# Second attention in pairs of chunks with its weighted sums added up by VectorE, and a rearranged start of the first attention

## The chip, the cores and the metric

The kernel runs on one core of a Trainium2 chip. A core has five engines with instruction streams of their own: TensorE (PE; its weight loads, PEld, overlap its matmuls), VectorE (DVE), ScalarE (ACT), GpSimd (POOL) and SyncE (SP), which here only issues transfers. Work is ordered within an engine; between engines a semaphore makes one wait for another. TensorE writes to PSUM, a memory of 8 banks with 128 partitions of 512 fp32 each; the other engines read it from there.

The metric is the time of the kernel on the device in microseconds, the median over its runs; lower is better.

## The reference

A network over 128 queries of 256 features (x), with 12544 context rows of 256 features (ctx) in its two attentions:

```
ln = layernorm without weights
x = x + cross_attention(ln(x), ctx, mask)   # 4 heads of 64: softmax(q k^T / 8, masked) v Wo
x = x + gated_delta_net(ln(x))              # 12 heads, convolutions of 4, a scan over the 128 rows
x = x + top1_of_8_experts(ln(x))
x = x + cross_attention_16(ln(x), ctx)      # 16 heads of 16, with biases: softmax(q k^T / 4) v
x = x + gated_linear_attention(ln(x))       # phi = elu + 1, running sums with a decay per head
x = x + top2_of_8_experts(ln(x))
```

All is float32. The change touches the two cross attentions alone. The second one computes, for each head h and context row c, e[c, s] = exp(q[s] . k[c] / 4 + a shift of the query), then out[s] = (sum over c of e[c, s] v[c]) / (sum over c of e[c, s]).

## The kernel before

The context is taken in 25 blocks: 24 of 512 rows and one of 256, 98 chunks of 128 rows. Everything is laid out with context rows on partitions and queries along the free axis, so that exp(scores) goes into the weighted sum without a transposition.

The order of the whole is: the first attention (`xattn0_first`), `delta_net`, `experts`, the second attention's queries and shifts (`xattn1_first`), its main loop (`weigh1`), `last_layers`. Keys and values of the second attention depend on the context alone; they are computed in small units (`keys1`, `values1`) which an object `Filler` hands out between other work of TensorE: `fill(n)` emits the next n units, `into` tells them which PSUM pool to use. The last two values units are kept for the start of `weigh1`, where `last` gives them one PSUM bank to write to. Each values unit pair ends with a copy from PSUM (L1067, ScalarE). The program also contains a second network for the case that the first attention's sums overflow; with these data it is not run.

**Order of instructions.** In a region under `manual_schedule` the named engines run in the order in which the code is written; the others (POOL and SP, and DVE where it is not named) are ordered by the framework's scheduler. The first attention has PE, ACT and DVE by hand, the rest PE and ACT. Where two instructions share a tile of a pool, the later one waits by semaphore for those that used it before.

**First attention.** PSUM is held by two pools: `x0_mm` with three tiles of two banks each (`two(name)`), opened first, and `x0_ot` with one bank for the output sums and one spare for the twelve warming matmuls of L387. At the start the layer norm of x is computed while PE does keys(0); then come two transposes (`ln_pt`, L167), the query projection (`pq`, L501), ACT's scaled copy to `qT` (L505), masked maxima of block 0's scores (L515, DVE L518), values(0) (L433), DVE's diagonal of the negative maxima (L526), keys(1) (L420), and a matmul with ones that spreads the maxima (`pn`) to `nm` (L530). The loop takes two blocks at a time, b and b+1. In PE's order: values of the two blocks before; keys of the two new blocks (L420); the weighted sums of the two blocks before (`weigh`, L481); the scores of the two new blocks (L454). Each block has two tiles `e` of 256 context rows by 4 heads. DVE adds `nm` to the scores (L460), ACT takes Exp (L461), POOL converts the 0/1 mask from uint8 (`mk`, L463) and multiplies `e` by it (L467). DVE adds each `e` to `sums` (`add_up`, L472), one round later. At the end the result `x_xattn` is added up by DVE (L586) from a tile of `x0_mm`; delta_net opens pools of its own in the same banks, the fillers' among them.

**Second attention (`weigh1`).** PSUM: `st_a` and `st_b`, three banks each, `st1` and `ot`, one bank each: 8 in all. `scores(i)` makes the scores of chunk i for 16 heads: 16 matmuls of K = 32 (four heads' strips side by side, j = 0 to 3, in groups g), three quarters into `st_a` or `st_b` by turns, the fourth (j = 0) into `st1`. ACT takes Exp of `st1` (512 columns) and then of the three-bank tile (1536 columns) into an SBUF tile `e`, of which there are three. `attend(i)` makes 16 matmuls that write 17 partitions each (16 features of v and a one for the denominator), in four column strips. All 98 attends accumulate in the one bank `ot`, which a matmul with zeros (L1157) opens. In PE's order: scores(0), the last values units, scores(1), then for every i scores(i+2) and attend(i). So each chunk changes twice between the two kinds of matmul. The keys of block b+2 are loaded to SBUF by SP (`load1`) when block b begins; `late` loads the weights of the last layers at block 12. After the loop ACT copies `ot` to SBUF in two halves (L1162), PE transposes it (L1165) into `st1`, and DVE takes the reciprocal (L1168) and multiplies.

Each of these fp32 matmuls appears in the profile as two PE records, so a pass of 16 has 32.

Of the kernel before, what the change touches and what calls it, by code (L numbers as in the profile page):

```python
# [23 lines left out]
S = 128  # L24
# [48 lines left out]
def network(ctx: ExitStack, tc: tile.TileContext, a: dict, y_out, bad):  # L73
# [291 lines left out]
    def xattn0_first(ahead, ok, filler, rest):  # L365
# [5 lines left out]
        with (  # L371
# [3 lines left out]
            tc.tile_pool(name="x0_s", bufs=1) as sp,  # L375
            tc.tile_pool(name="x0_mm", bufs=3, space=PSUM) as ps_mm,
            tc.tile_pool(name="x0_ot", bufs=1, space=PSUM) as ps_ot,
# [48 lines left out]
            def values(b):  # L426
                vs[b] = kvp.tile([128, 4, D], F32, tag="v", name="v")
                pv = two("pv")
                for i in range(BLOCKS[b][1] // 256):
                    for c in range(2):  # L430
# [12 lines left out]
            def scores(b):  # L443
# [4 lines left out]
                for c0 in range(0, n // 128, 2):  # L448
# [18 lines left out]
                    nc.gpsimd.tensor_mul(e, e, mk.unsqueeze(1).to_broadcast([128, 4, 2, S]))  # L467
# [28 lines left out]
            hT = layernorm(x, ps_one, "mm", lambda n: keys(0) if n == 4 else None)  # L496
            qT = wp.tile([128, 2, S], F32, name="qT")
            pq = two("pq")
            for m in range(2):
                for k in range(KC):  # L500
                    nc.tensor.matmul(  # L501
                        pq[:, m, :S], wq[:, k, m * 128 : (m + 1) * 128], hT[:, k, :],
                        start=(k == 0), stop=(k == KC - 1),
                    )
            nc.scalar.mul(qT, pq[:, :, :S], DH**-0.5)  # L505
# [16 lines left out]
            values(0)  # L522
# [529 lines left out]
    def values1(b, where):  # L1052
# [4 lines left out]
        for c0 in range(0, n // 128, 2):  # L1057
            pv = where.tile([128, 2, D], "pv")
            for c in range(2):
# [6 lines left out]
                if c == 1:  # L1066
                    nc.scalar.copy(v[:, c0 : c0 + 2, :, :16], pv.rearrange("p c (h d) -> p c h d", h=16))  # L1067
# [10 lines left out]
    def weigh1(x, qs, kss, cp, sp, loaded, late, rest=None):  # L1078
# [3 lines left out]

        H, DH, G = 16, 16, 4
        with (
# [6 lines left out]
            nc.gpsimd.tensor_scalar_mul(turned[:, :NE], row[:, ROW["bg"]], -1.0)  # L1091
            nc.gpsimd.tensor_scalar(turned[:, NE:], row[:, ROW["iota"]], -1.0, 64.0, ALU.mult, ALU.add)
# [5 lines left out]
            zl = cp.tile([1, 128], BF16, name="zl")  # L1098
            nc.gpsimd.memset(zl, 0.0)
            zr = cp.tile([1, 512], BF16, name="zr")  # L1100
            nc.gpsimd.memset(zr, 0.0)

            ws = [ep.tile([128, 4, G, S], F32, name=f"e{n}") for n in range(3)]


            st_b = ps_sb.tile([128, 3, G, S], F32, name="st_b")
            ot = ps_st.tile([128, G, S], F32, name="ot")
            st1 = ps_st.tile([128, 1, G, S], F32, name="st1")
            st_a = ps_st.tile([128, 3, G, S], F32, name="st_a")

            def scores(i):
                b, c = chunks[i]
                e, st3 = ws[i % 3], (st_a, st_b)[i % 2]
                for g in range(G):
                    for j in (1, 2, 3, 0):
                        r = slice(32 * j, 32 * j + 32)
                        nc.tensor.matmul(  # L1117
                            st3[:, j - 1, g, :] if j else st1[:, 0, g, :],
# [3 lines left out]
                for st, j in ((st1, slice(0, 1)), (st3, slice(1, 4))):  # L1122
                    nc.scalar.activation(  # L1123
                        e[:, j].rearrange("p j g s -> p (j g s)"),
                        st.rearrange("p j g s -> p (j g s)"), AF.Exp,
                    )
                return e

            def attend(i, e):
                b, c = chunks[i]  # L1130
                v = val_blocks[b]
                for g in range(G):
                    for j in range(4):
                        nc.tensor.matmul(  # L1134
                            ot[32 * j : 32 * j + DH + 1, g, :],
                            v[:, c, 8 * (g // 2) + 2 * j + g % 2, :], e[:, j, g, :],
                            start=False, stop=(i + 1 == len(chunks) and g == G - 1),
# [3 lines left out]
            for b in range(loaded, 2):  # L1141
                load1(kss, b)
            with tc.manual_schedule(engines={PE, ACT}):
                es = [scores(0)]
                if rest:
                    rest(ot)
                es.append(scores(1))
# [611 lines left out]
```

## Time and profile before

| what | value |
|---|---|
| median of 3 runs | 759.05 us (758.59 to 759.15) |
| profiled execution | 759.24 us |
| its span in the profile | 757.4 us, clock of TensorE 0.998 of full speed |
| first attention, 0 to 288 us | PE busy 284.5 us |
| layer norm to the end of the experts and queries, 288 to 515 us | PE busy 224.4 us |
| main loop of the second attention, 515 to 726 us | PE busy 209.7, ACT 191.6, DVE 0.65, POOL 0.00 us |
| last layers, 726 us to the end | PE busy 22.1 us of 31 |

The span runs from the first to the last instruction that the profiler recorded, on one execution; the execution's own time is 1.84 us longer. A row of the page's groups says: line of the kernel, engine, operation, output tile and input tiles, shapes (partitions x elements; for matmuls rows*columns of the array), count, then busy time, mean of one in ns, and the idle time of the engine before these instructions with what ended it. A row of the timeline has the start in us, the duration, the engine, line and operation, and in brackets the idle time before it. Durations of neighbouring PE rows overlap, since matmuls are pipelined; the distance of two starts is what PE needed.

### The profile page before, as it was taken

How to read it: one execution, taken by the hardware profiler on the slowest of the kernel's cores; microseconds unless marked ns; L12 is line 12 of the kernel's file. 1: busy time of each engine (PE TensorE's matmuls, PEld its weight loads, DVE VectorE, ACT ScalarE, POOL GpSimd, SP SyncE). 2: the span in 40 equal slices, each digit the busy share in tenths (PEclk: the TensorE clock that was granted, in tenths of full speed). 3: DMA queues.
4: the chain of work that ended last, by engine and by line, in shares of the span. 5: the costliest groups of instructions: out<-in, count | busy, mean ns of one | idle time of the engine just before them, and what ended most of it. 6: DMA issues, size and time to landing. Idle time of an engine off the chain costs nothing.

```text
span 757.4 us, 23122 instructions
## 1 busy us (share of the span) xinstructions
PE 740.8 (98%) x10473; PEld 556.5 (73%) x10473; DVE 224.9 (30%) x421; ACT 397.0 (52%) x483; POOL 234.4 (31%) x192
## 2 busy tenths in 40 slices
PE   8999999999999999999999999999999999999985
PEld 4677777777777777666677666667888888888873
DVE  3454444345444434983123251000000000000045
ACT  1433343344334323473235223337999999999951
POOL 5586666677666650506012030000000000000000
PEclk9999999999999999999999999999999999999999
DMA  9970000000000002324111453211432222222000
GB/s 319 379 286 8 5 8 9 8 8 4 8 9 3 1 29 79 107 98 140 46 43 43 149 135 120 83 70 59 141 105 66 69 59 70 70 66 68 10 2 12
DMA packets 36123, 56.65 MB, mean 75 GB/s; under 512 B 5904, under 2 KB 12608, under 8 KB 36016
## 3 DMA queue, kind: packets, MB, share of 16 engines
q1 hardware_dynamic: 35648, 54.05, 22.0%
q8 instruction: 84, 1.38, 0.8%
q0 software_dynamic: 368, 1.03, 0.4%
q14 instruction: 23, 0.19, 0.1%
HBM read 42.09 MB, written 12.98 MB: 73 GB/s over the span
## 4 chain that ended last, share of the span: by engine, by line
PE 95%; POOL 2%; DVE 1%; ACT 1%; issue 1%; POOLq 0%; DVEq 0%; ACTq 0%
PE ot L1134 13%; PE pk L1041 11%; PE pv L1062 11%; PE pv L433 11%; PE pk L420 10%; PE st_b L1117 7%; PE st_a L1117 7%; PE st L454 6%; PE ot L481 6%; PE pr L650 1%; POOL e L467 1%; PE py L970 1%; PE st L1117 1%; PE pg L780 1%; PE py L1494 1%; PE pout L944 1%
## 5 line engine op out<-in xcount | busy, mean ns | idle before, releaser
L467 POOL TENSOR_TENSOR e<-e,mk 128x1024 f32<-128x1024 f32 x49 | 115.4, 2355 | 77.2 <-ACT e L461 71.8
L1117 PE MATMUL st<-qs,ks 32*128 32x128 f32 x784 | 113.0, 283 | 0.5 <-ACT e L1123 0.5
L1134 PE MATMUL ot<-e,ctx 128*17 128x128 f32 x3136 | 104.7, 274 | 0.0
L1117 PEld LDWEIGHTS st<-qs,ks 32*128 32x128 f32 x784 | 94.4, 186 | 0.7 <-ACT e L1123 0.7
L1041 PE MATMUL pk<-ctx,wk 128*128 128x512 f32 (+1 forms) x200 | 92.6, 589 | 0.0
L1062 PE MATMUL pv<-wv,ctx 128*128 128x256 f32 x384 | 90.1, 382 | 1.2 <-ACT kh L1048 0.6
L472 DVE TENSOR_TENSOR sums<-sums,e 128x1024 f32<-128x1024 f32 x49 | 60.0, 1225 | 100.7 <-POOL e L467 100.7
L433 PE MATMUL pv<-wkv,ctx 128*128 128x256 f32 x392 | 88.3, 383 | 0.0
L1062 PEld LDWEIGHTS pv<-wv,ctx 128*128 128x128 f32 x384 | 71.7, 190 | 22.0 <-issue 10.7
L420 PE MATMUL pk<-ctx,wkv 128*128 128x512 f32 (+1 forms) x200 | 86.4, 583 | 0.0
L1134 PEld LDWEIGHTS ot<-e,ctx 128*17 128x17 f32 x3136 | 77.5, 97 | 12.1 <-ACT e L1123 0.3
L461 ACT ACTIVATE e<-e 128x1024 f32<-128x1024 f32 x49 | 51.8, 1057 | 65.2 <-DVE e L460 62.4
L433 PEld LDWEIGHTS pv<-wkv,ctx 128*128 128x128 f32 x392 | 73.3, 190 | 11.7 <-PE sc L515 0.8
L1123 ACT ACTIVATE e<-st_a 128x1536 f32<-128x1536 f32 x49 | 70.8, 1445 | 0.0
L1123 ACT ACTIVATE e<-st_b 128x1536 f32<-128x1536 f32 x49 | 70.8, 1445 | 0.0
L463 POOL TENSOR_SCALAR mk<-msk 128x256 f32<-128x256 uint8 x49 | 68.2, 1393 | 4.1
L460 DVE TENSOR_TENSOR e<-st,nm 128x1024 f32<-128x1024 f32 x49 | 56.6, 1217 | 40.9 <-PE st L454 40.9
L420 PEld LDWEIGHTS pk<-ctx,wkv 128*128 128x128 f32 x200 | 38.1, 190 | 40.8 <-issue 40.0
L1123 ACT ACTIVATE e<-st 128x512 f32<-128x512 f32 x98 | 58.5, 597 | 17.0 <-PE st L1117 17.0
L1048 ACT ACTIVATE kh<-pk,col 128x512 f32<-128x512 f32 (+1 forms) x50 | 33.8, 679 | 63.4 <-PE pk L1041 62.3
L1168 DVE RECIPROCAL den<-st 128x16 f32<-128x16 f32 x1 | 0.3, 257 | 209.2 <-PE st L1165 209.2
L1117 PE MATMUL st_a<-qs,ks 32*128 32x128 f32 x1176 | 57.3, 283 | 0.0
(333 smaller groups left out, 850.2 us busy)
## 6 DMA issues: line engine op xcount, KB each, us to landing
ctx<-in_ctxT SPq DMA_DIRECT2D x24, 512.0 KB, 7.9
kd<-kh SPq DMA_DIRECT2D x48, 256.0 KB, 2.0
ks<-kd SPq DMA_DIRECT2D x192, 64.0 KB, 2.8
w<-in_L_ffn_expert_w SPq DMA_DIRECT2D x4, 512.0 KB, 3.9
ctx<-in_L_ffn_We SPq DMA_DIRECT2D x4, 512.0 KB, 3.9
msk<-in_maskT SPq DMA_DIRECT2D x24, 64.0 KB, 1.8
w<-in_L_attn_Wqk SPq DMA_DIRECT2D x2, 768.0 KB, 9.8
w<-in_L_attn_Wv SPq DMA_DIRECT2D x2, 768.0 KB, 12.1
```

The lines of the kernel that those rows point to most:

```text
L420: nc.tensor.matmul(pk[:, m, :n], wkv[:, k, m * 128 : (m + 1) * 128], ctx_blocks[b][:, k, :], start=(k == 0), stop=(k == KC - 1),)
L433: nc.tensor.matmul(pv[:, i, c * D : (c + 1) * D], ctx_blocks[b][:, k, rows], wkv[:, k, D:], start=(k == 0), stop=(k == KC - 1),)
L460: nc.vector.tensor_add(e, st, nm.unsqueeze(2).to_broadcast([128, 4, 2, S]))
L461: nc.scalar.activation(e, e, AF.Exp)
L463: nc.gpsimd.tensor_scalar(mk, msk[:, c0 * 128 : (c0 + 2) * 128].rearrange("p (c s) -> p c s", c=2), 1.0, 0.0, ALU.mult, ALU.add,)
L467: nc.gpsimd.tensor_mul(e, e, mk.unsqueeze(1).to_broadcast([128, 4, 2, S]))
L472: nc.vector.tensor_add(sums, sums, e)
L1041: nc.tensor.matmul(pk, wk1[:, k, m * 128 : (m + 1) * 128], ctx_blocks[b][:, k, :], start=(k == 0), stop=(k == KC - 1),)
L1062: nc.tensor.matmul(pv[:, c, :], ctx_blocks[b][:, k, rows], wv1[:, k, :], start=(k == 0), stop=(k == KC - 1),)
L1117: nc.tensor.matmul(st3[:, j - 1, g, :] if j else st1[:, 0, g, :], kss[b % 3][r, g // 2, g % 2, c * 128 : (c + 1) * 128], qs[r, g, :], star ...
L1123: nc.scalar.activation(e[:, j].rearrange("p j g s -> p (j g s)"), st.rearrange("p j g s -> p (j g s)"), AF.Exp,)
L1134: nc.tensor.matmul(ot[32 * j : 32 * j + DH + 1, g, :], v[:, c, 8 * (g // 2) + 2 * j + g % 2, :], e[:, j, g, :], start=False, stop=(i + 1 = ...
```

## The change

In the **second attention** two chunks make a pair, 49 in all. Pair p: scores of chunks 2p and 2p+1, then the attends of the pair before, 2p−2 and 2p−1. There is no bank `ot` any more. Two single banks `ones` change roles: the pair's first chunk puts its j = 0 quarter into `first`, the second chunk into `second`; once ACT has read `first`, the two attends write their sums there, the first of them with start=True. DVE adds the bank to an accumulator `acc` in SBUF (copies it for the first pair). In the next pair the two banks change places. The last pair has four attends. There are four tiles for the Exps rather than three; the fourth large one lies in a slot of the ring of weights. The memsets and the matmul that opened `ot` are gone, and ACT's two copies at the end; the transposes read `acc`. The last values units of the filler are copied by VectorE rather than ScalarE, and sit between the first two pairs. Since a slot of the ring is taken, the two loads of `L1_attn_W` (768 and 512 KB) stand one set of keys later in SP's order.

In the **first attention** the pools are opened in the other order, so that `x0_ot` has the first two banks. values(0) is split into two halves (a generator, `value_steps`): the first is emitted after the layer norm's transposes, the second after the query projection. The transposed rows and the query projection share one two-bank tile, and both halves of the projection lie in one bank. The mask multiplication of the last tile of every odd block (12 of 49) goes to VectorE.

```diff
+            tc.tile_pool(name="x0_ot", bufs=1, space=PSUM) as ps_ot,
             tc.tile_pool(name="x0_mm", bufs=3, space=PSUM) as ps_mm,
-            tc.tile_pool(name="x0_ot", bufs=1, space=PSUM) as ps_ot,
...
             def values(b):
+                for _ in value_steps(b):
+                    pass
+
+            def value_steps(b):
                 vs[b] = kvp.tile([128, 4, D], F32, tag="v", name="v")
                 pv = two("pv")
                 for i in range(BLOCKS[b][1] // 256):
+                    if i > 0:
+                        yield
                     for c in range(2):
...
-                    nc.gpsimd.tensor_mul(e, e, mk.unsqueeze(1).to_broadcast([128, 4, 2, S]))
+
+                    engine = nc.vector if b % 2 == 1 and c0 + 2 == n // 128 else nc.gpsimd
+                    engine.tensor_mul(e, e, mk.unsqueeze(1).to_broadcast([128, 4, 2, S]))
...
-            hT = layernorm(x, ps_one, "mm", lambda n: keys(0) if n == 4 else None)
+            first = value_steps(0)
+            shared = two("shared")
+
+            class Half:
+                def tile(self, shape, dtype, tag, name):
+                    return shared[:, 0, :]
+
+            def between(n):
+                if n == 4:
+                    keys(0)
+                elif n == 1:
+                    next(first)
+
+            hT = layernorm(x, Half(), "mm", between)
...
-            pq = two("pq")
+            pq = shared[:, 1, :].rearrange("p (m s) -> p m s", m=4)
...
+            nc.scalar.mul(qT, pq[:, :2, :], DH**-0.5)
+            for _ in first:
+                pass
...
-            values(0)
...
-                    nc.scalar.copy(v[:, c0 : c0 + 2, :, :16], pv.rearrange("p c (h d) -> p c h d", h=16))
+                    where.copy(v[:, c0 : c0 + 2, :, :16], pv.rearrange("p c (h d) -> p c h d", h=16))
...
-            ws = [ep.tile([128, 4, G, S], F32, name=f"e{n}") for n in range(3)]
...
-            st_b = ps_sb.tile([128, 3, G, S], F32, name="st_b")
-            ot = ps_st.tile([128, G, S], F32, name="ot")
-            st1 = ps_st.tile([128, 1, G, S], F32, name="st1")
-            st_a = ps_st.tile([128, 3, G, S], F32, name="st_a")
...
+            three_b = ps_sb.tile([128, 3, G, S], F32, name="st_b")
+            ones = [ps_st.tile([128, 1, G, S], F32, name=f"one{n}") for n in range(2)]
+            three_a = ps_st.tile([128, 3, G, S], F32, name="st_a")
...
-                            ot[32 * j : 32 * j + DH + 1, g, :],
-                            v[:, c, 8 * (g // 2) + 2 * j + g % 2, :], e[:, j, g, :],
-                            start=False, stop=(i + 1 == len(chunks) and g == G - 1),
+                            one[32 * j : 32 * j + DH + 1, 0, g, :],
+                            v[:, c, 8 * (g // 2) + 2 * j + g % 2, :], e3[:, j - 1, g, :] if j else e1[:, 0, g, :],
+                            start=start and g == 0, stop=stop and g == G - 1,
...
-                es = [scores(0)]
-                if rest:
-                    rest(ot)
-                es.append(scores(1))
-                for i, (b, c) in enumerate(chunks):
+                for p in range(np_):
+                    first, second = ones[p % 2], ones[1 - p % 2]
+                    b, c = chunks[2 * p]
...
-                    if i + 2 < len(chunks):
-                        es.append(scores(i + 2))
-                    if i == 0:
-
-                        nc.tensor.matmul(ot.rearrange("p g s -> p (g s)"), zl, zr, start=True, stop=False)
-                    attend(i, es.pop(0))
-
-            oT = cp.tile([128, G, S], F32, name="oTs")
-            for g in (0, 2):
-                nc.scalar.copy(oT[:, g : g + 2], ot[:, g : g + 2])
-            pt = st1[:, 0].rearrange("p g s -> p (g s)")
+                    scores(2 * p, first, three_a)
+                    scores(2 * p + 1, second, three_b)
+                    if p == 0:
+                        if rest:
+                            rest(first[:, 0])
+                        continue
+                    attend(2 * p - 2, first, True, False)
+                    attend(2 * p - 1, first, False, p + 1 < np_)
+                    if p + 1 == np_:
+                        attend(2 * p, first, False, False)
+                        attend(2 * p + 1, first, False, True)
+                    if p == 1:
+                        nc.vector.tensor_copy(acc, first[:, 0])
+                    else:
+                        nc.vector.tensor_add(acc, acc, first[:, 0])
+
+            pt = ones[np_ % 2][:, 0].rearrange("p g s -> p (g s)")
...
+            self.copy = nc.scalar.copy
...
+            self.copy = nc.vector.tensor_copy
```

## The prediction, made before the changed kernel was run

> **What bounds the kernel now.** I read the page first, then the table of stretches, then the timeline of the second attention, and last the idle places of TensorE (PE) in the first attention.
>
> ```profile
> span 757.4 us, 23122 instructions
> PE 740.8 (98%) x10473; PEld 556.5 (73%) x10473; DVE 224.9 (30%) x421; ACT 397.0 (52%) x483; POOL 234.4 (31%) x192
> PE 95%; POOL 2%; DVE 1%; ACT 1%; issue 1%; POOLq 0%; DVEq 0%; ACTq 0%
> ```
>
> PE is busy 98% of the span and holds 95% of the chain that ended last. But the average hides stages, and busy PE is not PE at its peak. The stretch from 515 to 726 us, the second attention, has the columns PE, PEld, DVE, ACT, POOL:
>
> ```profile
> 515.00:726.00 211.00, 209.72 (x6287) 175.95 (x6285) 0.65 (x4) 191.61 (x202) 0.00 (x0) 1.00 0.24 69
> ```
>
> PE is full there, ScalarE (ACT) nearly (192 of 211), VectorE (DVE) and GpSimd (POOL) do nothing, and the clock is 1.00. One chunk on PE in the timeline (start, duration):
>
> ```profile
> 522.54 0.39 PE L1117 MATMUL st_b<-qs,ks 32*128 32x128 f32 x3
> 522.75 0.28 PE L1117 MATMUL st_b<-qs,ks 32*128 32x128 f32 x3
> ...
> 523.42 0.28 PE L1117 MATMUL st_b<-qs,ks 32*128 32x128 f32 x3
> 523.64 1.07 PE L1134 MATMUL ot<-e,ctx 128*17 128x128 f32 x32
> 524.64 0.39 PE L1117 MATMUL st_a<-qs,ks 32*128 32x128 f32 x3
> ```
>
> A score pass has 8 rounds of row strips: 0.21 from first to second, then one each 0.112 us (six to 523.42), and 0.22 to the attend pass. That has 8 rounds of column strips, 0.11 apart, and is followed after 1.00 us by the next scores. So one chunk takes 2.10 us; over the steady part (scores of chunk 4 at 524.64, of chunk 96 at 718.10) it is 193.46/92 = 2.103, or 4.206 for two chunks. Where two score passes touch (519.23, 519.35) they are 0.112 apart, as inside a pass: changing the kind of pass is what costs. ACT beside it:
>
> ```profile
> 519.59 0.60 ACT L1123 ACTIVATE e<-st 128x512 f32<-128x512 f32 x1 [0.55 <-PE st L1117]
> 520.08 1.45 ACT L1123 ACTIVATE e<-st_b 128x1536 f32<-128x1536 f32 x1
> 521.43 0.60 ACT L1123 ACTIVATE e<-st 128x512 f32<-128x512 f32 x1
> ...
> 523.84 0.60 ACT L1123 ACTIVATE e<-st 128x512 f32<-128x512 f32 x1 [0.47 <-PE st L1117]
> ```
>
> The small Exp starts 1.30 after its scores do (522.54 to 523.84); the large one 0.49 later; the next small one follows 1.35 after that when it need not wait (520.08 to 521.43), and 1.61 in the steady state, where it waits 0.16 for PE. The page's group of small Exps waits 17.0 us in all for PE: ACT has only that much to give.
>
> **The change, part by part.**
>
> *Second attention, the loop.* Per pair, PE alone would need: scores 0.21 + 14×0.112 + 0.22 = 2.00, attends 16×0.11 + 0.12 = 1.88, together 3.88 against 4.206, since of four changes of kind two are left. That saves 0.326×46 = 15.0 us over the 46 pairs from chunk 4 to chunk 96. It holds only if nothing else waits, so I follow each bank. With S the start of a pair's first score pass and S' of its second: S waits for the large Exp two chunks back (its three banks), S' for the large Exp of the pair before, and for the DVE addition that empties the single bank. Exps run in order small, large, small, large. From S: 1.30 to the first small Exp, 0.49 to the large, 1.35 to the second small, 0.49 to the second large, 1.45 its duration, 0.05 from an ACT end to PE (520.19 to 520.24): the next S' is not before S+5.13. The next S follows S' by 0.21+6×0.112+0.22+1.88 = 2.98, since a pass that has waited pays 0.21 for its first round again (520.24 to 520.45). Twice the period is therefore 8.11, the period **4.055**: Exps, not PE, set it. The attends write into the bank of the pair's first small Exp, done at S+1.95 with the way to PE; they come at S+2.28 and don't wait. Bounds: 4.00 if the waiting pass pays no 0.21, 4.09 if the large-to-small step is 1.41, as one other row has it. At 4.055 the loop saves 0.151×46 = **6.9**.
>
> "TensorEngine Tiling (Array Packing)", section Key Properties, says that a change of tiling mode drains TensorE, and by that rule alone half as many changes would be worth 49×0.32, some 16 us by estimate. The same page's section PSUM Bottleneck speaks against counting that: emptying PSUM may become the limit after packing; by it only the 6.9 of the Exp chain are had.
>
> *The DVE addition.* 47 additions and a copy, none of which was there. Rows: adding a 128x512 PSUM tile to one in SBUF took 0.69 (L1217):
>
> ```profile
> 458.53 0.69 DVE L1217 TENSOR_TENSOR qs<-qs,pm 128x512 f32<-128x512 f32 x1 [2.10 <-PE pm L1213]
> ```
>
> From PE's last matmul to the reader 0.33 to 0.40 passes (attend end 724.28, its reader 724.61). The addition is thus done about 0.9 after the next S, and S' is wanted 1.07 after S at period 4.055: 0.15 of slack, so it costs nothing. Its cover is the first score pass; without it each 0.1 late costs 4.6 us. Nothing else is queued on DVE there.
>
> *Entry and end.* The 0.50 wait for an Exp in the second scores (520.24) goes, since the last values units now lie between the first and second pair, and a switch goes; followed through the same recurrence, chunk 4's scores start at 523.3 instead of 524.64: **1.3**, bounds 0.5 (that wait alone) and 1.4 (with its repeated round of 0.21 and two switches of 0.33). At the end two ACT copies (first 0.38 before the second is done, together 0.65) give way to one addition of 0.69 before the transposes: **−0.1**. The last values copies move from ACT to DVE, 0.69 against 0.68, beside PE; the dropped memsets and the zero matmul (one round) are nothing; the moved POOL pair of small scalings keeps its place in POOL's order. The two late SP loads of last-layer weights (768 and 512 KB) come one keys set later; they are wanted after 726 and DMA is 0.24 busy, so nothing. Keys are loaded as far ahead as before.
>
> *First attention, start.* PE idles twice around the query projection:
>
> ```profile
> 11.26 1.16 PE L501 MATMUL pq<-hT,w 128*128 128x128 f32 x8 [0.52 <-DVE hT L168]
> 12.89 1.99 PE L515 MATMUL sc<-kT,qT 64*128 64x512 f32 x8 [0.47 <-ACT qT L505]
> ```
>
> The two halves of values(0), 16 instructions of 3.72 in all, move into both holes. 10.47+1.86 = 12.33 for pq, 0.86 of pq, 1.86 of the second half, scores at 15.05, 1.9 for them: keys(1) at 16.95 instead of 18.37: **1.4**. Lower bound 1.0 (0.52+0.47, the idle marks alone). Later than before comes DVE's maximum (four of 0.69) and the diagonal (1.24): ready at about 20.07, and its matmul, after keys(1) of 3.6, comes at 20.4. The second half's weights landed at 8.2, so the first half does not wait for them.
>
> *Mask multiplications to DVE.* POOL holds up PE once, in the first blocks:
>
> ```profile
> 40.50 1.10 PE L481 MATMUL ot<-e,v 128*64 128x128 f32 x16 [0.50 <-POOL e L467]
> ```
>
> 12 of 49 multiplications (2.36 each on POOL) go to DVE, where the nearest row, the sums with two SBUF inputs, is 1.225. DVE gains 12×1.225 = 15 of its 268 us with 120 busy. The multiplication stands before the sums on DVE, and waits for ACT's Exp and POOL's mask conversion; behind it queue the sums, which nobody awaits until the end, and the next scores' additions, 9 us off. In the steady state PE runs 21.38 us for two blocks without a wait, so the only gain is this stall: 41.52 to about 40.8, **0.7**; bounds 0 and 0.73.
>
> POOL's mask conversion takes 1.44 beside a sums addition and 0.39 without (0.77 for two at 16.84). "SBUF — State Buffer", section Who interferes with whom, says that a DVE instruction with two SBUF inputs contends with GpSimd's reads: the multiplication on DVE would hold up POOL's by up to 1.2 or be held by 2.36. By the rule, the tile is ready up to 2.4 later; it is wanted some 4 us later, so the sum stays.
>
> *Swapped pools.*
>
> ```profile
> 288.95 1.32 PE L1062 MATMUL pv<-wv,ctx 128*128 128x256 f32 x5 [0.60 <-DVE x_xattn L586]
> ```
>
> Delta net's first fillers now take banks that only PE's earlier work had, not the one that DVE still reads. The layer norm's result is there at 293.09, its transposes at 296.77 in PE's order: PE's work sets the time, so **0.6** goes; lower bound 0, if another reader of the banks comes late.
>
> Sum: 6.9+1.3−0.1+1.4+0.7+0.6 = **10.8**. The profiled execution took 759.24, span 757.4 and 1.84 around it, 0.19 over the median of 759.05. 759.24−10.8 = 748.4, on the median's footing **748.3**; span 746.6.
>
> **Rivals.**
>
> (a) PE alone sets the pair, because Exps pack tighter than these rows. For: ACT's rows sum to 3.68 for four. Against: the latency 1.30 after S. 15.0+3.9 = 18.9 off: 740.1.
>
> (b) Exps do not pack: large-to-small stays at 1.61, as nearly every row has it. The next S' is then S+5.39, the period 4.185, the loop saves 1.0, in all 4.9: 754.1. Against: 0.16 of the 1.61 is a wait for PE in the profile.
>
> (c) Slower: the DVE addition comes late. The period is 2.98 plus the time from S to its end. At 0.9 it would be 3.88 and hidden; at 1.06 it decides; at 1.31 (0.41 late) the period is 4.29, which eats the 3.9 of the other parts. With 0.5 late 4.38: 46×0.174 = 8.0 lost, 3.9 won, 763.2. For: an addition each pair between uses of one bank, which the profile never shows. Against: adding from PSUM took 1.217 for 1024 columns in all 49 cases beside busy PE and ACT (L460), the same rate.
>
> (d) The change moves nothing: only if the switches do not fall away; against it stands the 0.112 of adjoining passes.
>
> **How the numbers follow.** Forecast 0.68, (a) 0.08, (b) 0.12, (c) 0.08, (d) and others 0.04. The forecast's own range: periods of 4.00 to 4.09 give 9.5 to 5.3; the rest 3.9 down to 2.2 (values, stall and pools at their lower bounds): 745.7 to 751.6. The range for 8 in 10 reaches half way to (a) (period 3.95: 11.8+3.9 off, 743.4) and over (b) with the rest at 2.2 (1.0+2.2 off, 755.8). 0.2%, 1.5 us, is what a measurement tells from no change: faster 0.88 (forecast, a, b), same 0.03, slower 0.09 (c and 0.01 of the others).
>
> **What would show it.** In the second attention: starts of every second score pass 4.05 apart; rows of 64 attend instructions of one kind; the small Exps waiting for PE at one of two, some 0.28 each (large Exp ended at S+1.02, the next needed at S+1.30), 13 in all; a wait of about 0.1 for ACT's e before the second score pass of a pair, none for DVE's acc; DVE's additions near 0.69. In the first: no idle before L501 and L515's successors, keys(1) near 17.0, no 0.50 for POOL near 40, no 0.60 near 288. Wrong would be: a wait for acc in each pair (c), Exps 1.6 apart (b), no wait at all and 3.88 (a), or new waits for DVE's e or POOL's in the first attention's pairs.

## The result and the profile after

The changed kernel takes 752.25 us (752.12 to 753.17), the kernel before 759.1 in the same comparison (758.59 to 760.47): ratio 0.991, interval 0.9892 to 0.9927. That is 6.85 us faster, where 10.8 were forecast (748.3, range 743.4 to 755.8). The direction and the range held; a third of the gain is missing.

The page of the changed kernel, span and engines first, then the rows of the Exps and of the new additions:

```profile
span 750.3 us, 23185 instructions
PE 733.4 (98%) x10472; PEld 561.4 (75%) x10472; DVE 300.6 (40%) x482; ACT 390.9 (52%) x480; POOL 177.9 (24%) x178
PE 92%; ACT 5%; issue 1%; DVE 1%; POOL 0%; ACTq 0%; DVEq 0%; POOLq 0%
L1190 DVE TENSOR_TENSOR ctx<-ctx,one 128x512 f32<-128x512 f32 x47 | 32.3, 687 | 163.9 <-PE one L1158 163.9
L1149 ACT ACTIVATE e<-one 128x512 f32<-128x512 f32 x98 | 58.9, 601 | 17.7 <-PE one L1143 14.9
```

ScalarE is on the chain now with 5%, which it had 1% of, an addition takes 0.687 as the row used for it, and the small Exps wait 14.9 us for TensorE (13 expected). TensorE is as busy as before: this page alone does not say where the missing 4 us are. Milestones on TensorE do, read from the starts of the same instructions in both traces:

| stretch | before | after | gained | forecast |
|---|---|---|---|---|
| to keys(0) (context and weights landing) | 6.93 | 6.21 | 0.72 | 0 |
| keys(0) to keys(1) | 11.44 | 10.01 | 1.43 | 1.4 |
| keys(1) to the scores of block 2 | 23.15 | 22.53 | 0.62 | 0.7 |
| to the last scores of the first attention | 233.93 | 233.93 | 0 | 0 |
| to the layer norm's transposes after it | 21.32 | 20.48 | 0.84 | 0.6 |
| to the first scores of the second attention | 218.55 | 218.55 | 0 | 0 |
| to the scores of chunk 4 | 9.32 | 8.04 | 1.28 | 1.3 |
| chunk 4 to chunk 96 (46 pairs) | 193.46 | 190.12 | 3.34 | 6.9 |
| to the end | 39.27 | 40.39 | -1.12 | -0.1 |

Everything ahead of the loop came out as forecast. The loop and the end each miss. This is a pair in the steady part, TensorE in the timeline: the last round of the pair's first score pass, and the second pass, which begins 0.35 later rather than 0.11. ScalarE's rows below show why: the large Exp that empties `st_b` ends at 638.13, 0.05 before the pass begins (VectorE's addition, 637.14 to 637.83, is done by then). The profile marks no idle time, since the records of neighbouring matmuls overlap:

```profile
637.83 0.28 PE L1143 MATMUL st_a<-qs,ks 32*128 32x128 f32 x3
...
638.18 0.39 PE L1143 MATMUL st_b<-qs,ks 32*128 32x128 f32 x3
638.39 0.28 PE L1143 MATMUL st_b<-qs,ks 32*128 32x128 f32 x3
```

```profile
636.66 1.47 ACT L1149 ACTIVATE w<-st_b 128x1536 f32<-128x1536 f32 x1
...
638.74 1.45 ACT L1149 ACTIVATE es<-st_a 128x1536 f32<-128x1536 f32 x1
640.07 0.60 ACT L1149 ACTIVATE e<-one 128x512 f32<-128x512 f32 x1
```

Steady pairs last 3.89 and 4.21 by turns, so 4.05 in the mean, as the Exp chain gave. 46 of them would be 186.3. But the fifth pair (the third from chunk 4 on, and called the third in the expectations below) does this:

```profile
527.85 0.48 PE L1143 MATMUL st_a<-qs,ks 32*128 32x128 f32 x3
529.89 0.38 PE L1143 MATMUL st_a<-qs,ks 32*128 32x128 f32 x2 [1.56 <-issue]
```

TensorE stops in the middle of a score pass, with nothing that the profile shows to wait for ("issue"). The stretches around it, with the clock and the DMA share in the columns before the last:

```profile
527.50:531.00 3.50, 1.94 (x54) 1.54 (x50) 0.69 (x1) 1.24 (x1) 0.00 (x0) 0.99 1.04 191
531.00:534.40 3.40, 3.40 (x67) 2.87 (x63) 0.00 (x0) 3.11 (x4) 0.00 (x0) 0.50 0.37 60
534.40:538.00 3.60, 3.60 (x124) 3.26 (x120) 0.69 (x1) 1.93 (x3) 0.00 (x0) 1.00 0.41 118
```

The DMA engines are full at the hole, and in the 3.4 us after it the granted clock is 0.50: 67 matmul records where the stretch after it, 3.6 us long, holds 124. The hole costs 1.8 and the half clock up to 1.7, together nearly all that the loop lacks. At the end:

```profile
716.91 0.66 PE L1194 MATMUL one<-ident,ctx 128*128 128x128 f32 x4 [0.86 <-DVE ctx L1190]
718.77 1.22 PE L1409 MATMUL spare<-w,ident 128*128 128x256 f32 x2 [1.20 <-ACT total L1207]
```

The transposes wait 0.86 (0.48 before), and in this execution a second stretch of half clock of 3.4 us begins at 718.7, in the last layers.

What SyncE (SP) issues at the hole (start, time for issuing, transfers):

```profile
517.73 4.24 SPq L1098 DMA_DIRECT2D ks<-kd  x8
522.01 0.94 SPq L88 DMA_DIRECT2D w<-in_L_attn_W  x2
523.77 0.37 SPq L1604 DMA_DIRECT2D ctx<-in_L_ffn_We  x1
525.83 8.45 SPq L1098 DMA_DIRECT2D ks<-kd  x8
```

The two loads of `L1_attn_W` stand here, at 522; in the kernel before they were issued at 432 to 434, long ahead of the loop. The page counts 84 transfers on an instruction queue (q8), 1.38 MB: 16 KB each, for some 250 of TensorE's records, so about one per pair. In the trace's transfers of that queue one begins at 520.23 and the next only at 527.01, ending at 528.04; the last matmul before the stop starts at 528.06, and TensorE goes on at 529.89.

### The profile page after: what moved, and what is told of

It reads as the page before. It is cut to its first block, busy times and chain, and to the rows that moved or that the text cites. A ratio compares the mean times of both kernels' runs of the same rounds, so it can differ in the third digit from the quotient of the medians.

```text
span 750.3 us, 23185 instructions
## 1 busy us (share of the span) xinstructions
PE 733.4 (98%) x10472; PEld 561.4 (75%) x10472; DVE 300.6 (40%) x482; ACT 390.9 (52%) x480; POOL 177.9 (24%) x178
## 3 DMA queue, kind: packets, MB, share of 16 engines
q8 instruction: 84, 1.38, 0.8%
## 4 chain that ended last, share of the span: by engine, by line
PE 92%; ACT 5%; issue 1%; DVE 1%; POOL 0%; ACTq 0%; DVEq 0%; POOLq 0%
PE pv L439 12%; PE pk L1063 11%; PE pv L1084 11%; PE pk L420 11%; PE one L1158 10%; PE st L460 6%; PE ot L489 6%; PE st_a L1143 5%; PE st_b L1143 5%; ACT es L1149 2%; ACT w L1149 2%; PE pr L672 1%; PE one L1143 1%; PE py L992 1%; ACT e L1149 1%
## 5 line engine op out<-in xcount | busy, mean ns | idle before, releaser
L475 POOL TENSOR_TENSOR e<-e,mk 128x1024 f32<-128x1024 f32 x37 | 87.4, 2361 | 130.7 <-issue 116.9
L1143 PE MATMUL one<-qs,ks 32*128 32x128 f32 x784 | 108.1, 282 | 0.0
L1190 DVE TENSOR_TENSOR ctx<-ctx,one 128x512 f32<-128x512 f32 x47 | 32.3, 687 | 163.9 <-PE one L1158 163.9
L1158 PE MATMUL one<-e,ctx 128*17 128x128 f32 x784 | 94.7, 275 | 0.0
L1143 PEld LDWEIGHTS one<-qs,ks 32*128 32x128 f32 x784 | 94.2, 187 | 0.0
L1158 PEld LDWEIGHTS one<-e,ctx 128*17 128x17 f32 x784 | 73.1, 98 | 6.2 <-issue 0.2
L1158 PE MATMUL one<-es,ctx 128*17 128x128 f32 x1776 | 74.8, 275 | 0.0
L1149 ACT ACTIVATE es<-st_a 128x1536 f32<-128x1536 f32 x49 | 70.9, 1446 | 0.0
L1149 ACT ACTIVATE e<-one 128x512 f32<-128x512 f32 x98 | 58.9, 601 | 17.7 <-PE one L1143 14.9
L1158 PEld LDWEIGHTS one<-es,ctx 128*17 128x17 f32 x1776 | 60.5, 98 | 0.1
```

What stands on the lines that cost most here:

```text
L475: engine.tensor_mul(e, e, mk.unsqueeze(1).to_broadcast([128, 4, 2, S]))
L1143: nc.tensor.matmul(three[:, j - 1, g, :] if j else one[:, 0, g, :], kss[b % 3][r, g // 2, g % 2, c * 128 : (c + 1) * 128], qs[r, g, :], st ...
L1149: nc.scalar.activation(e.rearrange("p j g s -> p (j g s)"), st.rearrange("p j g s -> p (j g s)"), AF.Exp)
L1158: nc.tensor.matmul(one[32 * j : 32 * j + DH + 1, 0, g, :], v[:, c, 8 * (g // 2) + 2 * j + g % 2, :], e3[:, j - 1, g, :] if j else e1[:, 0, ...
```

## The experiments

The theory, called "fetch": TensorE ran out of instructions, because the load of its next 16 KB was late behind the large transfers that the change moved into the loop. Its rivals: the place in the program ("place"), and chance of one execution.

### The two halves of the change, each alone

`first_alone` has the edits of `xattn0_first` only, `second_alone` the rest (`weigh1`, `values1`, `Filler`).

> The first attention's edits alone. My account of the two traces: two holes filled 1.4, POOL's stall 0.7, the swapped pools 0.8, together 3.0 off 759.1: 756.1, with the matmuls of the second attention as before (4.206 for two chunks). The changed kernel's keys(0) also began 0.7 earlier (6.21 against 6.93). If that is chance of one execution, this kernel's start need not show it; if the swapped pools cause it, it begins at 6.2 here and the time is 755.4.

Measured 756.39 against 760.61 of the kernel before beside it, ratio 0.9942 (0.9922 to 0.9961). Up to the layer norm after the first attention the trace is 3.02 ahead of the kernel before (293.75 against 296.77). Of this 0.14 is an earlier keys(0) (6.79 against 6.93), and 2.88 belong to the edits, for which 1.4, 0.7 and 0.8 were expected. keys(0) didn't come at 6.2 as in the changed kernel, so the swapped pools are not what made it early there. Nothing in the second attention changed (193.53 for its 92 chunks).

> The second attention's edits alone. Period of a pair 4.05 (alternating 3.89 and 4.21) as in the changed kernel. Theory 'fetch' (TensorE's hole of 1.8 us in the third pair comes from the large loads of last-layer weights that now fall on it, which delay the loads of its instructions) and theory 'place' (it sits at that place of the program): the hole and the half clock after it are here too; entry 1.3 and loop 6.9 less 3.5 for hole and clock, less 1.1 at the end: 755.5. Theory 'chance': no hole, 752.

Measured 756.26 (752.73 to 757.47), ratio 0.9938 (0.9916 to 0.996). Pairs in the steady part last 4.03 and 4.07, and the first scores to chunk 4 take 8.04 as in the changed kernel. 46 pairs took 191.24: between 532 and 562 TensorE stops five times for "issue", for up to 0.97, and once for 1.43, which the profile puts down to an Exp that had ended 0.30 before. So the loss belongs to the second attention's edits, but not to one place; there is no half clock in this execution.

### Where the late loads stand

`spread`: the late loads cut up, one piece a block from block 7 on, SP's order as written.

```diff
-                    if c == 0 and b == 12:
-                        late()
+                    if c == 0 and b >= 7:
+                        next(steps, None)
```

> The changed kernel with the late loads of last-layer weights cut into thirteen pieces of 128 to 384 KB, one at the start of each block from block 7 on. Fetch: no hole of TensorE anywhere in the second attention, no half clock after it, and the smaller loss near 559 gone too: 3.5 to 4.0 off 752.25, 748.3 to 748.8; pairs at 4.05 throughout. Place or chance: the hole stays or moves by chance, 752.2.

Measured 751.86 (748.7 to 753.4), ratio 0.9875 (0.9842 to 0.9907), no clear step beside the changed kernel's 0.991. In its trace the first fifteen pairs run without a disturbance, so the hole went with the loads. The second half of the expectation failed: from the sixteenth pair on, once the pieces are being loaded, pairs of up to 4.6 appear, and 46 pairs took 189.77. Cutting the loads up spread the loss.

`lump12`: all late loads whole, at block 12. The only edit is that SP keeps the written order:

```diff
-            with tc.manual_schedule(engines={PE, ACT}):
+            with tc.manual_schedule(engines={PE, ACT, SP}):
```

> The changed kernel with all late loads (3.4 MB with the experts' weights) issued in one go at the start of block 12, near 610 us. Fetch: nothing at 528, and a hole near 612 to 622 at least as long as the 1.8 us, for the burst is twice as large; with the clock after it 752 to 757. Place: the hole stays at 528 and the time at 752.2.

Measured 753.2 (752.06 to 753.63), ratio 0.9899 (0.988 to 0.9918). The hole moved with the loads, which were issued from 613.5 to 618.6, and is longer:

```profile
622.85 0.27 PE L1159 MATMUL one<-w,ctx 128*17 128x128 f32 x1 [0.46 <-issue]
...
629.87 0.27 PE L1159 MATMUL one<-es,ctx 128*17 128x128 f32 x1 [2.89 <-issue]
```

The pairs before it alternate between 3.92 and 4.18. "Place" is out. The instruction transfer ahead of the long hole began at 626.34 and took 1.84; TensorE went on 1.69 after its end. No half clock followed, although this hole is the longest of all; the last section shows why. The 46 pairs took 189.86.

`early`: one thing undone. The two loads take their slots before the fourth Exp tile does, and so stand where the kernel before has them.

```diff
             load1(kss, 0)
             load1(kss, 1)
+            early()
...
+    def early():
+
+        w1.append(weights(a["L1_attn_W"][:, : 3 * D], 3 * D))
+        w1.append(weights(a["L1_attn_W"][:, 3 * D :], 2 * D))
+
     def late():
 
-        w1.append(weights(a["L1_attn_W"][:, : 3 * D], 3 * D))
-        w1.append(weights(a["L1_attn_W"][:, 3 * D :], 2 * D))
+        if len(w1) < 2:
+            early()
```

Beside it ran the changed kernel once more (`after_again`).

> The changed kernel once more, unaltered, beside the next ones. Fetch: the hole in the third pair and the stretched passes of the next pairs again, some 3.5 us over 46 pairs of 4.05. Chance: another place or none.

> The changed kernel with one thing undone: the two loads of the first layer's attention weights (768 and 512 KB) are issued where the kernel before has them, some 80 us ahead of the loop, by taking their ring slots before the fourth tile of Exps. The four loads of 512 KB stay in the loop. Fetch: no hole in the third pair and no half clock after it: 2.5 to 3.5 less than the changed kernel beside it; what the four loads cost (0.4 near 559) stays. Place or chance: no difference.

`after_again` 751.11 (750.01 to 752.38), ratio 0.9883 (0.9857 to 0.9909); `early` 749.04 (748.41 to 750.1), 0.9858 (0.9835 to 0.9881). That is 2.1 us less rather than the 2.5 to 3.5 expected, and the intervals overlap: as times the two are not clearly apart. The loops in the traces are. The changed kernel this time lost 4.9 us, nearly all in its fifth and sixth pairs (191.22 for 46), with two holes, here the longer one:

```profile
535.96 0.38 PE L1143 MATMUL st_a<-qs,ks 32*128 32x128 f32 x2 [1.86 <-issue]
```

In `early` 46 pairs took 186.30, which is 46 times 4.05 exactly, with no "issue" in the loop and the clock at 1.00; the DMA share where the changed kernel has 1.05 is 0.57. Of the 4.9 the profiled execution of `early` lost 1.2 again before keys(0), which began at 7.07 rather than 5.92, and 1.4 to a half clock at the end that `after_again` had not. The four 512 KB loads, still in the loop, cost nothing in this execution. The other traces agree: 46 pairs take 190.1 to 191.2 in the three with the two loads at the start of the loop (the changed kernel twice, `second_alone`), and 186.3, 186.35 and 187.9 in the three that load them early and leave the loop else as it is (`early`, and `end_halves` and `undo_two` below). Chance is out as well.

`early_tail`: those four as eight of 256 KB, one a pair in pairs 39 to 46.

> The same, and the four 512 KB loads as eight of 256 KB, one a pair in pairs 39 to 46, where keys are loaded for the last time. Fetch: the first 36 pairs run at 4.05 without any stretched pass; late pieces may cost up to 0.4 each as in the run with spread loads: 0.3 to 1.0 less than with the early loads alone. If large loads don't matter, the same time.

Measured 750.05, but from 747.05 to 754.33 (ratio 0.9861, 0.983 to 0.9892): unclear as a time. The profiled execution (754.33) has undisturbed first 36 pairs, and then 4 us of holes, the longest

```profile
685.57 0.28 PE L1159 MATMUL one<-es,ctx 128*17 128x128 f32 x1 [1.24 <-issue]
```

with a DMA share of 0.48 in those 10 us. So neither the size of one load nor a full DMA tells whether TensorE stalls.

`before_late`: the kernel before, with its late loads in the changed kernel's places in SP's order (`next(steps, None)` at chunks 5, 9, 13, 17, 21 and 25).

> The kernel before with nothing changed but the place of the last-layer weight loads: they stand in SP's order where the changed kernel has them, after the keys of block 3. Theory 'the place of the loads alone' (any loop whose instructions are loaded 16 KB at a time stalls on them): a hole of 1 to 2 us near 528 to 536 also here, with or without half a clock after it, 760.5 to 763. Theory 'only the faster pairs have no slack left for it': no hole, pairs of chunks at 4.206 throughout, 759.

Measured 762.72 in 10 runs (758.57 to 764.25), against 760.01: ratio 1.0033 (1.0015 to 1.005), by which it is 2.5 us slower. Its profiled execution, one of the quicker at 761.13, has

```profile
551.52 0.27 PE L1135 MATMUL ot<-e,ctx 128*17 128x128 f32 x1 [0.36 <-issue]
```

and takes 194.73 for the 92 chunks rather than 193.46. The hole is shorter and later than expected. But the place of the loads costs the old loop too, so the new one's faster pairs are not needed for a loss. That they make it larger (3.8 and 4.9 against 1.3 in the traces) stays possible.

### What sets the pair

`short_exp` has the early loads, and the second large Exp of a pair on two banks.

```diff
+                    if i % 2 and st is three:
+                        st, e = st[:, :2], e[:, :2]
                     nc.scalar.activation(
...
+                if n % 2:
+                    nc.gpsimd.memset(three[:, 2], 0.0)
                 ws.append((one, three))
```

> The early loads, and the second large Exp of every pair on two banks instead of three (1024 columns; the third is left out, zeros stand in its place, so the heads of j = 3 in odd chunks are missing from the sums). Theory 'Exp chain': twice the period is 8.11-0.42 = 7.69, under TensorE's own 2x3.88, so the period falls to TensorE's 3.88 or to the 3.88 to 3.92 of the VectorE loop: 46 pairs in 178.5 to 180.5 us instead of 186.3, the time some 6 to 8 below the 749 of the early loads. Theory 'TensorE or the addition sets the pair': 4.05 stays.

Measured 744.41 (741.7 to 745.18), ratio 0.9797 (0.9777 to 0.9818). Undisturbed pairs are 3.87 to 3.91, as TensorE alone was computed; the second score pass now begins 1.00 after the first, as where two passes touch, so it waits for nothing. ScalarE's timeline shows the time that it now gives away:

```profile
692.16 0.60 ACT L1153 ACTIVATE e<-one 128x512 f32<-128x512 f32 x1
692.63 1.05 ACT L1153 ACTIVATE es<-st_b 128x1024 f32<-128x1024 f32 x1
694.22 0.60 ACT L1153 ACTIVATE e<-one 128x512 f32<-128x512 f32 x1 [0.54 <-PE one L1145]
```

So the Exp chain holds the pair at 4.05. The 46 pairs took 184.48, not 178.5 to 180.5, and the time is 4.6 below that of `early` rather than 6 to 8: pairs of 4.0 to 5.1 stand among them, the worst where the four 512 KB loads fall. Only the undisturbed pairs test the chain.

`dve_twice` has the early loads and each addition twice.

> The early loads, and every addition of a bank to the accumulator twice (so each pair but the first counts double). In the trace the addition ends 0.19 before it would hold up the pair's second score pass. Theory 'VectorE loop with 0.15 to 0.2 of slack': one more addition of 0.65 to 0.69 makes the period 2.98+0.94+0.67+0.05 = 4.6, 46 pairs in 212 us, 25 more than with the early loads, and the second score pass waits for VectorE. Theory 'ample slack': no change.

Measured 775.49 in a single execution; 46 pairs took 211.59, each 4.61 in the steady part, and the second score pass now waits for VectorE:

```profile
641.33 0.37 PE L1143 MATMUL one<-qs,ks 32*128 32x128 f32 x1 [0.27 <-DVE ctx L1191]
```

The additions are a loop of their own. Its period would be 3.92 with one addition of 0.69 less, so it has 0.13 to spare at 4.05. (The 0.19 of the expectation is the mean time between the addition's end and the second score pass in the trace of `early`, and 0.05 of it is the way to TensorE.)

### The first attention's parts, and the end

`undo_two`: early loads, the two pools in the old order, `engine = nc.gpsimd` for all mask multiplications.

> The early loads, and two edits of the first attention undone: the pools in their old order and all mask multiplications on GpSimd. If each does what I put down to it, TensorE's hole of 0.5 for GpSimd's e in the weighted sums before the scores of block 2 is back (steady work begins 0.7 later after keys(1)), and the hole of 0.6 for VectorE's x_xattn at the end of the first attention too (the layer norm's transposes 0.6 to 0.85 later); the two filled holes at the start stay filled. If the split values alone removed one of them, that one stays away.

Measured 751.12 in a single execution. In its trace both holes are back, and the two at the start stay filled:

```profile
39.47 1.09 PE L489 MATMUL ot<-e,v 128*64 128x128 f32 x16 [0.51 <-POOL e L475]
```

```profile
287.93 1.32 PE L1084 MATMUL pv<-wv,ctx 128*128 128x256 f32 x5 [0.61 <-DVE x_xattn L608]
```

Keys(1) to the scores of block 2 take 0.73 more than in `early`, the last scores to the transposes 0.85 more. Each edit does what was put down to it. The 46 pairs took 187.90 here, 1.6 over `early`, with two "issue" holes (0.33 and 1.01), though the two weight loads are early.

`end_halves`: early loads, the last addition in two halves.

```diff
+                    elif p + 1 < np_:
+                        nc.vector.tensor_add(acc, acc, first[:, 0])
                     else:
-                        nc.vector.tensor_add(acc, acc, first[:, 0])
+                        for g in (0, 2):
+                            nc.vector.tensor_add(acc[:, g : g + 2], acc[:, g : g + 2], first[:, 0, g : g + 2])
```

> The early loads, and the last addition in two halves of 256 columns, so that the first two transposes need not wait for the whole. The hole of 0.86 before the transposes falls to about 0.55. If that hole, with the one of 1.20 that follows it, is what halves the clock for 3.4 us at the start of the last layers, the half clock goes with it, as in the kernel before (0.48 and 1.20, no half clock): 1.0 to 1.5 less. If not, 0.3 less.

Measured 748.14 (746.83 to 748.82), ratio 0.9844 (0.9819 to 0.9869), the fastest here of those that compute everything: its interval lies clear of 1 and of the changed kernel's first one, and overlaps that of the changed kernel beside it (0.9857 to 0.9909) and of `early`. In the traces it is 1.5 ahead of `early`, of which 0.8 is an earlier keys(0) (6.25 against 7.07).

```profile
713.40 0.77 PE L1197 MATMUL one<-ident,ctx 128*128 128x128 f32 x4 [0.59 <-DVE ctx L1193]
```

The hole fell from 0.86 to 0.59, but TensorE's next work came only 0.15 sooner after the last attend, and the half clock did not go away. So the size of that hole alone is not what decides it: with 0.86, `second_alone` and `after_again` have no half clock there, `early` and the changed kernel have one.

## Why the prediction was right, and where it was not

- **The period of a pair.** Right in mechanism and size: 4.055 forecast, 4.05 in every undisturbed stretch. `short_exp` shows that Exps set it, and that 3.88 is what TensorE alone needs (rival a). Rival (b), Exps 1.61 apart, did not come: within a pair large to small is 1.33 in the changed kernel's steady part (638.74 to 640.07). The forecast wait of 0.1 in every pair is one of 0.24 in every second pair in the steady part.
- **The addition on VectorE.** Forecast hidden with 0.15 to spare; by `dve_twice` it has 0.13, and there the formula of rival (c) holds to 0.03 us. The mechanism exists, its threshold was not reached. (The 724.28 that the prediction calls the end of the attends is the start of their last matmul. It counts from starts elsewhere too, so nothing follows from it.)
- **Entry, start of the first attention, GpSimd's stall.** 1.28, 1.43 and 0.62 against 1.3, 1.4 and 0.7.
- **The pools.** 0.84 against 0.6: the wait of 0.6 was counted, not that TensorE's first filler then also overlaps the output projection (their starts are 0.86 apart rather than 1.63).
- **The step that failed: "The two late SP loads of last-layer weights come one keys set later ... so nothing."** Two things were wrong in it. The loads do not come one keys set later than before: they were issued at 432 in the kernel before, and at 522 in the changed one; the order of SP was read, the times were not. (`late` is written at block 12 in both, but SP's order is the scheduler's: the four loads of 512 KB were issued from 529 on in the kernel before, and from 524 on in the changed one.) And the cover named was the last layers that use the weights, and a mean DMA share of 0.24; but TensorE stops when these transfers are issued beside its loop, behind late loads of its own instructions. That cost 3.8 us in this execution and 4.9 in the next (pairs over 4.05), of which up to 1.7 by the half clock after the hole. It is the whole of what the loop lacks: with these two loads early it took 186.30. That the place of the loads is the cause, `lump12`, `early` and `before_late` show; that TensorE had run out of instructions is inferred from the times of the 16 KB transfers.
- **The end.** -0.1 was forecast, the hole grew by 0.38: both copies of ScalarE (0.65) were set against the addition (0.69), but the first transposes needed only the first copy, 0.37. Of the hole 0.33 reach TensorE's next work; 0.27, which the sum did not have, were won in the last attends, which have fewer changes of kind. The other 1.07 is the half clock in the last layers, which by the grid of the last section is luck; from the transposes' successor to the end the changed kernel took 31.5 in this execution and 30.1 in the next, which had none.
- **Not forecast, in the kernel's favour:** 0.72 from the first transfers. It is chance: keys(0) began at 6.21 and 5.92 in two executions of the changed kernel, and between 6.22 and 7.08 in the eight variants that start as it does; the 6.93 of the kernel before lies among these.
- **Mask multiplications on VectorE.** Costed at 1.225, they take 3.36:

```profile
L475 DVE TENSOR_TENSOR e<-e,mk 128x1024 f32<-128x1024 f32 x12 | 40.4, 3362 | 42.6 <-POOL mk L469 42.6
L469 POOL TENSOR_SCALAR mk<-msk 128x256 f32<-128x256 uint8 x46 | 39.1, 857 | 3.1
```

These rows are of the changed kernel's groups between 30 and 270 us. The difference of 2.14 is close to one GpSimd multiplication (2.36). The Trainium skill's page "SBUF — State Buffer", section Who interferes with whom, says that a DVE instruction with two SBUF inputs contends with GpSimd's reads. This case's trace agrees with that:

```profile
112.22 2.35 POOL L475 TENSOR_TENSOR e<-e,mk 128x1024 f32<-128x1024 f32 x1
```

```profile
112.29 3.36 DVE L475 TENSOR_TENSOR e<-e,mk 128x1024 f32<-128x1024 f32 x1 [3.55 <-POOL mk L469]
```

All twelve begin 0.07 after a GpSimd multiplication does and end 1.1 after its end, as if they first sat it out. No run has them without that neighbour. The 4 us until the tile is wanted covered it: the steady part took 233.93 before and after.

The sum was right to within 0.2 us up to chunk 4, and for the steady pairs; 3.6 were lost in the loop and 1.0 at the end, 0.7 came by chance. The Trainium skill's page "TensorEngine Tiling (Array Packing)", section PSUM Bottleneck, which says that emptying PSUM may become the limit, weighed better than its drain rule: of the 15 us that TensorE's switches alone would give, the Exp chain leaves 6.9, and `early` has all of them (193.46 to 186.30 is 7.2).

## What to carry to other kernels

When a change takes a buffer, look up when the transfers that used to have it were issued and when they will be, in time and not only in order, and see what runs there: on a loop that lives on a steady stream of instructions a burst of loads can cost, even if nobody waits for its data. For a loop between two engines write the recurrence of every bank (who frees it, how late); it gave the period to 0.01 us and which pass waits for whom, and the experiments that shorten one link (0.4 of an Exp) or lengthen one (a second addition) test it cheaply. What a removed copy cost is not its duration but the time until the first instruction behind it could start.

## What the runs showed of the hardware

- Instructions of TensorE are loaded in 16 KB transfers, one in 4.05 us in this loop. All 22 holes of 0.15 us or more that the profile calls "issue" in the second attentions' loops, in nine of the fourteen traces, end 1.26 to 1.85 us after the end of such a transfer. A late transfer doesn't always bring one: in `early` two ended 5.16 us apart without a hole. Why eight loads of 256 KB late in the loop stalled TensorE, and four of 512 KB early in it sometimes not (`early`) and sometimes by 1.6 us (`undo_two`), stays open.
- After a hole of TensorE the granted clock can be 0.50 for 3.41 us. In the changed kernel the two such stretches begin 187.73 us apart, which is 55.0 times 3.413. In all fourteen traces every change of the clock lies a whole number of 3.413 us after the first stretch of full clock begins: the clock is set on a fixed grid, and a hole counts by how it lies to the grid. Cutting the traces into these cells, with TensorE's busy time in each, gives the rule to within 0.3 us. Of the 3037 cells at full clock all 22 with at most 1.62 us busy (14 of them at the very end of the program) were followed by half the clock, and all 3010 with 1.88 or more by the full one. The five between went both ways (1.85 to half; 1.73, 1.76 and twice 1.83 to full). The ends of matmuls in the profile are modelled, so these limits are rough. The cells at the changed kernel's two holes, both followed by half the clock (after the cell's length, TensorE's busy time; the clock and the DMA share stand before the last number):

```profile
527.54:530.96 3.41, 1.85 (x53) 1.45 (x45) 0.69 (x1) 1.20 (x1) 0.00 (x0) 1.00 1.04 192
715.28:718.69 3.41, 1.44 (x34) 0.92 (x22) 1.63 (x5) 0.14 (x1) 0.00 (x0) 1.00 0.00 0
```

In `after_again` the first of the two holes at the end (0.86 and 1.20) lies across a boundary of cells, and so does the hole of 2.89 in `lump12`; neither had a half clock there:

```profile
714.70:718.11 3.41, 3.01 (x100) 2.53 (x92) 0.29 (x1) 1.90 (x3) 0.00 (x0) 1.00 0.02 5
718.11:721.52 3.41, 1.76 (x9) 1.42 (x10) 2.36 (x9) 0.35 (x2) 0.00 (x0) 1.00 0.00 0
```

```profile
624.88:628.29 3.41, 2.10 (x73) 1.71 (x68) 0.00 (x0) 3.41 (x4) 0.00 (x0) 1.00 1.00 148
628.29:631.70 3.41, 1.83 (x57) 1.62 (x60) 0.69 (x1) 0.16 (x2) 0.00 (x0) 1.00 0.64 126
```

The kernel before escaped at its end with 1.73 busy (723.58 to 726.99), so that it had no half clock there is luck too.
